# Second attention's keys and values projected inside the self-attention units, and token norms with one reciprocal root

## The chip, the cores and the metric

The kernel runs on one core of a Trainium2 chip. The core has a matrix engine (PE, with its weight loads shown as PEld), a vector engine (DVE), a scalar engine (ACT), a general engine (POOL), a synchronizing engine (SP) that here only issues transfers, and 16 DMA engines that all queues share. The metric is the device time of one execution in microseconds. Before the change it is 1516.2 us, the median of three runs from 1514.5 to 1518.3.

## What is computed

The input x is 16 batches of 128 tokens with 256 features; a context of the same shape comes with it. Four layers each add a gated branch to x, and each begins with a layer norm of x without weights:

```python
# first branch: gated attention over LN(x) (self) and over the context (cross)
ln_out = _ln(hidden_states, ln_w, ln_b)          # hidden_states is _layernorm(x): a norm of a norm
q = _ln(_fp8_linear_pertensor(ln_out, wq, ...))  # 16 heads of 128, 8 key groups; k, v likewise
core = _gqa(q, k, v)                             # self
xout = _gqa(qx, kx, vx)                          # cross: keys and values are cond @ w_kv_x
return catq(concat[core, xout]) @ wproj * ...
# second branch: feed-forward with ternary weights, silu(g) * u
# third branch: causal attention, 32 heads of 8, keys and values from the context
q = (Q @ w_q.T).reshape(B, S, G, HG, HD)         # G = 8 groups, HG = 4 heads, HD = 8
k = (K @ w_k.T).reshape(B, S, G, HD)             # 64 key features in all
v = (V @ w_v.T).reshape(B, S, G, HD)
# fourth branch: each token to one of 8 experts of bounded capacity
```

The keys and values of the third branch depend on the context and on weights only, not on x.

## The kernel before

The program has four stages, one after the other, which overlap at their seams.

**Gated attention.** The work is cut into 32 units: unit u is batch u % 16, the first 16 for self-attention and the last 16 for cross-attention. A loop over n runs from -11 to 135, and a unit advances by four steps. At each step the loop body issues parts of several units: projections of one unit (`project`, L422, into a ring of two PSUM banks, `ps_mm`), evictions by ACT (`evict`, L431 and L434), statistics of heads (`bn`, L443), the heads' reciprocal roots (`rstd`, L448 to L464), the heads' scaling by POOL (`mult`, L474), their transposes (`heads`, L485, L494), scores (L503, into a ring of two banks, `ps_sc`), their maxima (L511), exponentials (L519), the division (L527, L531), transposes and values (L539, L541, L549), the smoothing and rounding to eight bits (L560, and the helper `e4m3` whose last POOL step is L237 and whose result is called `cat`), and the output projection (`output`, L590). Weights are fetched in tiles called `stage` and split in two parts. The order on each engine is made by a scheduler that starts from this program order and moves an instruction ahead of others when its operands are ready earlier; so a part put at one place of the loop body can come to stand elsewhere on its engine.

Each self unit begins with a norm of its tokens. `stats` (L302 to L324) does the statistics of four batches at once, at n = -11, 5, 21 and 37. Since the reference takes a norm of a norm, it computes two reciprocal roots, the second from the variance that is left after the first, and multiplies them. A reciprocal root is made by `rsqrt` (L181 to L191): ACT takes the logarithm (L185) and an exponential of minus half of it (L186) as an estimate, and DVE improves that in four small steps (L187 to L190). All of its tiles lie in SBUF. The heads' reciprocal roots in `rstd` are made in another way: the estimate lies in a bank of the scores' PSUM ring and DVE needs three steps (L462 to L464).

Cross units fetch the context of their batch in `load` (L346) into a ring of two tiles, `ctx`.

**Feed-forward.** Four groups of four batches; `gate_up` and `down`. PE has no gaps here. SP fetches the weights of the next stage in these steps, among them `aq`, `ak`, `av`, `ao`.

**Second attention.** Groups of four batches. `front_step` spreads what a group needs over the steps before it: `load` (L931 to L945: the context of the group, called `cT`, issued on POOL's queue, and the mask, on SP's queue, from which DVE makes the tile `comb`), `norm`, `turn`, and then `qk` in four calls: two chunks of 128 query features and two chunks of 128 key features, each two matmuls of 128x512 (L982) and an ACT eviction (L987 for queries, L989 for keys). The key weights `ak` are laid out with every group's eight features repeated for its four heads, so the 64 key features fill 256 rows. For every batch `keys` masks the keys for four heads by POOL (L1000, result `kb`), projects the values with two matmuls (L1006) and writes them by four DVE copies (L1011) to a padded tile `vpad`, of which there are two; the zeros between stay from the start. A step of the main loop then makes eight heads' scores (L1022, L1029), maxima (L1036), exponentials (L1045), transposes (L1056, L1057) and, every second step, values (L1072) and their division (L1078, L1079); after a batch's last step the output projection (L1085). Routing of tokens to experts runs in between.

**Experts.** Eight of them, with transfers of their weights.

Of the change, these lines of the loop matter most: the place in the body behind which the new work is put.

```python
            if ab[1]:
                ab[1][0].project(ab[1][1])
                ab[1][0].evict(ab[1][1])
                ab[1][0].bn(ab[1][1])
            do(n, 5, "output")
```

Of the kernel before, what the change touches and what calls it, by code (L numbers as in the profile page):

```python
# [9 lines left out]
F32 = mybir.dt.float32  # L10
# [5 lines left out]
ALU = mybir.AluOpType  # L16
# [19 lines left out]
def flamingo_kernel(  # L36
# [206 lines left out]

    xqx = dram.tile([B, P, KD * P], F32, name="xqx")
    x1 = dram.tile([B, P, DM], F32, name="x1")
    NU = 2 * B


# [2 lines left out]
    with (  # L251
# [37 lines left out]
        def load_proj(cross, q):  # L289
# [7 lines left out]
                split(st, None, dst[:, c : c + n, 0, :], dst[:, c : c + n, 1, :])  # L297
            wpr[cross, q] = dst

        norms = {}  # L300

        def stats(g):  # L302

            xg = ap.tile([P, 4, DM], F32, tag="xg", name="xg", bufs=1)
            nc.sync.dma_start(
                out=xg, in_=x_in[4 * g : 4 * g + 4].rearrange("b s d -> s b d")
            )
            mv = small.tile([P, 4, 2], F32, tag="mv0", name="mv0", bufs=2)
            for j in range(4):
                stx = small.tile([P, 6], F32, tag="st0", name="st0")  # L310
                nc.vector.bn_stats(stx, xg[:, j, :])
                nc.vector.bn_aggr(mv[:, j, :], stx)
            v1 = small.tile([P, 4], F32, tag="v1", name="v1", bufs=1)
            nc.vector.tensor_scalar(v1, mv[:, :, 1], EPS, None, ALU.add)
            r1 = rsqrt(small, v1, 4, "x1", 1)
            v2 = small.tile([P, 4], F32, tag="v2", name="v2", bufs=1)
            nc.vector.tensor_tensor(v2, r1, r1, ALU.mult)
            nc.vector.tensor_tensor(v2, v2, mv[:, :, 1], ALU.mult)
            nc.vector.tensor_scalar(v2, v2, EPS, None, ALU.add)
            r2 = rsqrt(small, v2, 4, "x2", 1)  # L320
            rr = small.tile([P, 4], F32, tag="rr", name="rr", bufs=2)
            nc.vector.tensor_tensor(rr, r1, r2, ALU.mult)
            for j in range(4):
                norms[4 * g + j] = (xg[:, j, :], mv[:, j, 0:1], rr[:, j : j + 1])  # L324

        class Unit:
# [118 lines left out]
            def rstd(self):  # L445

                st = self.st
                var = small.tile([P, 24], F32, tag="q_var", name="q_var", bufs=1)  # L448
                dif = small.tile([P, 24], F32, tag="q_dif", name="q_dif", bufs=1)
                nc.vector.tensor_tensor(dif, st[:, :, 1], st[:, :, 4], ALU.subtract)  # L450
                nc.vector.scalar_tensor_tensor(dif, dif, 0.25, dif, ALU.mult, ALU.mult)
                nc.vector.scalar_tensor_tensor(
                    var, st[:, :, 2], P * EPS, st[:, :, 5], ALU.add, ALU.add
                )
                nc.vector.scalar_tensor_tensor(var, var, 1.0 / P, dif, ALU.mult, ALU.add)

                a = small.tile([P, 24], F32, tag="q_a", name="q_a", bufs=2)
                est = ps_sc([P, 24])
                self.r = small.tile([P, 24], F32, tag="q_r", name="q_r", bufs=2)
                nc.scalar.activation(a, var, AF.Ln)  # L460
                nc.scalar.activation(est, a, AF.Exp, scale=-0.5)
                nc.vector.scalar_tensor_tensor(a, est, -0.5, var, ALU.mult, ALU.mult)  # L462
                nc.vector.tensor_tensor(a, est, a, ALU.mult)
                nc.vector.scalar_tensor_tensor(self.r, a, 1.5, est, ALU.add, ALU.mult)  # L464

            def mult_q(self, c):
                self.mult(c + 2)
# [143 lines left out]
        units = [Unit(u) for u in range(NU)]  # L611


        loads = {}

        def at(n, f, *args):
# [34 lines left out]
        for n in range(first, last + 1):  # L651
            for m in range(0, B, 4):
                if n == 4 * m - 11:
                    stats(m // 4)
            once(n, -8, "load")
            for f, args in loads.get(n, ()):
                f(*args)
            ab = [front(n, i) for i in range(2)]
            do(n, 1, "recip")
            do(n, 4, "quant_last")  # L660
            do(n, 1, "divide")
            do(n, 0, "scores")
# [12 lines left out]
            for blk in range(2):  # L675
                once(n, -2, "mult", blk)
                once(n, -1, "heads", blk)
            do(n, -2, "mult_q")
            do(n, -1, "heads_q")
            do(n, 3, "quant")  # L680
            if ab[1]:
                ab[1][0].project(ab[1][1])
                ab[1][0].evict(ab[1][1])
                ab[1][0].bn(ab[1][1])
            do(n, 5, "output")
            once(n, 8, "residual")
# [197 lines left out]
    cq = f1.enter_context(tc.tile_pool(name="a1c", bufs=1, side="right", reuse_waits="tile"))  # L884
    gp = f1.enter_context(tc.tile_pool(name="a1f", bufs=2, side="right", reuse_waits="tile"))
    aq = cq.tile([P, KD, DM], F32, name="aq")
    ak = cq.tile([P, KD, DM], F32, name="ak")
    av = cq.tile([P, KD, NG * HD], F32, name="av")
    ao = cq.tile([P, KD, DM], F32, name="ao")
    bo = cq.tile([P, DM], F32, name="bo")  # L890
    nc.sync.dma_start(out=aq, in_=kpn(aqT))
    nc.sync.dma_start(out=ak, in_=kpn(akT))
    nc.sync.dma_start(out=av, in_=kpn(avT))
    nc.sync.dma_start(out=ao, in_=kpn(aoT))
    nc.sync.dma_start(out=bo, in_=b_o.partition_broadcast(P))

# [32 lines left out]
    front = {}  # L929

    def load(g):  # L931
        cT = gp.tile([P, KD, NT], F32, tag="cT", name="cT")
        nc.gpsimd.dma_start(out=cT, in_=kpn(ctxT)[:, :, g * NT : (g + 1) * NT])
        mi = gp.tile([P, NT], I32, tag="mi", name="mi", bufs=1)
        nc.sync.dma_start(
            out=mi, in_=mask[g * NT : (g + 1) * NT].partition_broadcast(P)
        )
        comb = gp.tile([P, G, P], BF16, tag="comb", name="comb")
        pad = gp.tile([P, NT], F32, tag="pad", name="pad", bufs=1)
        nc.vector.tensor_scalar(pad, mi, 0.0, NEG, ALU.is_equal, ALU.mult)  # L940
        nc.vector.tensor_tensor(
            comb, pad.rearrange("p (b t) -> p b t", b=G),
            causal[:, None, :].to_broadcast([P, G, P]), ALU.min,
        )
        front[g] = {"cT": cT, "comb": comb}  # L945

    def norm(g):
        rows = [x[b] for b in range(g * G, (g + 1) * G)]
# [22 lines left out]
            nc.scalar.copy(hT[:, k, :], pt.rearrange("p n t -> p (n t)"))  # L971
        front[g]["hT"] = hT

    def qk(g, i, c):

        f = front[g]
        if c == 0:
            f[i] = gp.tile([P, KD, NT], F32, tag="qk"[i], name="qk"[i] + "T")
        w, src = ((aq, f["hT"]), (ak, f["cT"]))[i]
        pm = psum.tile([P, NT], F32, tag="mm", name="ps_mm")  # L980
        for k in range(KD):
            nc.tensor.matmul(  # L982
                pm, w[:, k, c * P : (c + 1) * P], src[:, k, :],
                start=(k == 0), stop=(k == KD - 1),
            )
        if i == 0:
            nc.scalar.activation(f[i][:, c, :], pm, AF.Copy, scale=SCALE1)  # L987
        else:
            nc.scalar.copy(f[i][:, c, :], pm)  # L989

    kbs, vps, es, eTs, oTs, scs, mxs = {}, {}, {}, {}, {}, {}, {}

    def keys(b):

        g, j = divmod(b, G)
        f = front[g]
        tok = slice(j * P, (j + 1) * P)
        kb = ap.tile([P, KD, NQ, P], F32, tag="kb", name="kb")
        for c in range(KD):
            nc.gpsimd.tensor_tensor(  # L1000
                kb[:, c], f[1][:, c, None, tok].to_broadcast([P, NQ, P]),
                hmask[:, :, None].to_broadcast([P, NQ, P]), ALU.mult,
            )
        pm = psum.tile([P, NG, HD], F32, tag="mm", name="ps_mm")
        for k in range(KD):
            nc.tensor.matmul(  # L1006
                pm, f["cT"][:, k, tok], av[:, k, :], start=(k == 0), stop=(k == KD - 1)
            )
        vp = vpads[b % 2]
        for i in range(NQ):  # L1010
            nc.vector.tensor_copy(vp[:, :, i, HD * i : HD * i + HD], pm)  # L1011
        kbs[b], vps[b] = kb, vp

    def scores(n):

# [10 lines left out]
        with tc.high_priority(offset=100):  # L1026
            for i in range(2):
                rows = slice(32 * (2 * p + i), 32 * (2 * p + i) + 32)
                nc.tensor.matmul(  # L1029
                    s[:, i], f[0][rows, c, tok], kbs[b][rows, c], start=False, stop=True  # L1030
                )
        scs[n] = s

# [64 lines left out]
    def front_step(g, i):  # L1098

        if i == 0:  # L1100
            load(g)
            norm(g)
        elif i == 3:
            turn(g)
        elif 5 <= i < 9:
            qk(g, (i - 5) // 2, (i - 5) % 2)

    hds = {}
    for g in range(B // G):
# [182 lines left out]
```

## Time and profile before

| what | value |
|---|---|
| median of three runs | 1516.2 us (1514.5 to 1518.3) |
| the profiled execution | 1515.79 us, its span 1514.1 us |
| mean granted PE clock | 0.974 |
| busy: PE, DVE, ACT, POOL | 91%, 68%, 54%, 44% of the span |
| PE busy in 300 to 400 us (self-attention) | 91.92 us |
| PE busy in 560 to 900 us (cross-attention) | 333.13 us of 340 |
| PE busy in 960 to 1000 us (feed-forward) | 40.00 us |
| PE busy in 1200 to 1300 us (second attention) | 99.86 us |

The span is what the profiler saw from the first to the last instruction; the execution's time has a little around it. Busy time counts instructions at work, not waits. Where PE is busy all the time, what it does sets the pace; where it has gaps, some wait does, and the lists of waits say which. Rows of the profile name an engine, a line of the program, the operation, and the tiles written and read. The time that an instruction takes and the spacing to the next of its kind can differ, since matmuls overlap.

### The profile page before, as it was taken

To read this page: it belongs to the slowest core of one execution; us is meant where nothing else is said; L and a number is where in the kernel's file an instruction comes from. 1 tells how busy PE (TensorE), PEld (TensorE's weight loads), DVE (VectorE), ACT (ScalarE), POOL (GpSimd) and SP (SyncE) were. 2 spreads that over 40 slices of the span, in tenths; PEclk is the share of its full clock that TensorE was granted. 3 is DMA by queue.
4 is the path that set the end of the run, shared out by engine and by line. 5 is a ranking of instruction groups with operands and counts; after the bars stand their busy time and mean duration, and the time that the engine had idled before them with its cause. 6 is when DMAs were issued, how large, how long until landed. Compare 5 with 4: busy or idle time off the path is not lost. (4 is left out here: it accounts for less than half of the span.)

```text
span 1514.1 us, 24690 instructions
## 1 busy us (share of the span) xinstructions
PE 1381.9 (91%) x8612; PEld 1004.0 (66%) x8612; DVE 1022.1 (68%) x2756; ACT 810.6 (54%) x2421; POOL 672.7 (44%) x574
## 2 busy tenths in 40 slices
PE   2789899898988999999999987999999999996998
PEld 1477677677766777777777764555556565654887
DVE  8988878786887876767777664533678787882100
ACT  3666666666666766666666651543445454542121
POOL 4577676777667455565655553120121311111111
PEclk9799999999999999999999998999999999996999
DMA  4301001000031100000000006200300100012662
GB/s 120 118 8 32 15 15 32 11 19 15 22 91 50 49 26 11 18 15 18 15 15 19 5 8 194 61 0 0 112 22 8 50 9 36 9 40 66 202 195 64
DMA packets 51116, 68.69 MB, mean 45 GB/s; under 512 B 5291, under 2 KB 37739, under 8 KB 50992
## 3 DMA queue, kind: packets, MB, share of 16 engines
q1 hardware_dynamic: 36912, 41.31, 9.0%
q10 hardware_dynamic: 11456, 17.63, 3.6%
q0 software_dynamic: 2624, 8.16, 1.5%
q8 instruction: 69, 1.13, 0.3%
q14 instruction: 55, 0.45, 0.1%
HBM read 50.53 MB, written 16.81 MB: 44 GB/s over the span
## 5 line engine op out<-in xcount | busy, mean ns | idle before, releaser
L531 POOL TENSOR_TENSOR e<-e,sums 128x512 f32<-128x512 f32 x128 | 139.7, 1091 | 226.7 <-DVE sums L527 108.8
L474 POOL TENSOR_TENSOR raw<-raw,q_r 128x512 f32<-128x512 f32 x192 | 211.9, 1129 | 19.8 <-DVE q_r L464 18.9
L519 ACT ACTIVATE e<-ps_sc,mx 128x128 f32<-128x128 f32 x512 | 181.4, 369 | 65.0 <-DVE mx L511 56.5
L443 DVE BATCH_NORM_STATS2 q_st<-raw 128x6 f32<-128x128 f32 x768 | 174.0, 278 | 61.7 <-ACT raw L434 61.3
L1045 ACT ACTIVATE e<-ps_sc,mx 128x128 f32<-128x128 f32 x512 | 139.7, 383 | 117.5 <-DVE mx L1036 106.4
L590 PE MATMUL ps_acc<-wp,cat 128*128 128x512 f32 x512 | 159.4, 433 | 27.4 <-POOL cat L237 26.9
L237 POOL TENSOR_TENSOR cat<-e_t,e_e 128x1024 fp32r<-128x1024 bf16 x64 | 136.3, 2129 | 47.4 <-DVE e_t L231 47.4
L541 ACT COPY eT<-ps_tr 128x512 f32<-128x512 f32 x128 | 75.4, 589 | 151.7 <-PE ps_tr L539 151.6
L503 PE MATMUL ps_sc<-kT,qT 128*128 128x128 f32 x1024 | 140.4, 280 | 17.1 <-ACT qT L494 17.1
L503 PEld LDWEIGHTS ps_sc<-kT,qT 128*128 128x128 f32 x1024 | 131.0, 193 | 35.4 <-ACT qT L494 28.7
L1000 POOL TENSOR_TENSOR kb<-kT,hmask 128x512 f32<-128x512 f32 x32 | 33.6, 1068 | 243.8 <-PE ps_sc L1029 184.5
L590 PEld LDWEIGHTS ps_acc<-wp,cat 128*128 128x128 f32 x512 | 94.7, 191 | 69.6 <-POOL cat L237 35.9
L549 PE MATMUL ps_pv<-eT,vt 128*128 128x256 f32 x512 | 132.8, 381 | 1.0 <-DVE cat_y L560 1.0
L485 PE MATMUL ps_tr<-ident,raw 128*128 128x128 f32 x768 | 115.4, 277 | 16.1 <-POOL raw L474 14.2
L434 ACT COPY raw<-ps_mm 128x512 f32<-128x512 f32 x192 | 114.0, 594 | 26.6 <-PE ps_mm L422 24.1
L485 PEld LDWEIGHTS ps_tr<-ident,raw 128*128 128x128 f32 x768 | 91.9, 142 | 50.4 <-POOL raw L474 23.5
L549 PEld LDWEIGHTS ps_pv<-eT,vt 128*128 128x128 f32 x512 | 96.5, 190 | 31.5 <-issue 11.4
L560 DVE TENSOR_TENSOR cat_y<-ps_pv,r_sm 128x512 bf16<-128x512 f32 x128 | 86.9, 679 | 39.9 <-PE ps_pv L549 39.7
L511 DVE TENSOR_REDUCE mx<-ps_sc 128x4 f32<-128x512 f32 x128 | 87.1, 680 | 36.5 <-PE ps_sc L503 35.9
L494 ACT ACTIVATE qT<-ps_tr,hv 128x512 f32<-128x512 f32 x128 | 101.1, 790 | 17.5 <-PE ps_tr L485 15.5
L519 ACT ACTIVATION_READ_ACCUMULATOR e<-ps_sc,mx 128x1 f32 x512 | 105.7, 206 | 0.0
L1036 DVE TENSOR_REDUCE mx<-ps_sc 128x8 f32<-128x1024 f32 x64 | 78.1, 1221 | 25.6 <-PE ps_sc L1029 23.5
(227 smaller groups left out, 2769.0 us busy)
## 6 DMA issues: line engine op xcount, KB each, us to landing
w1t<-in_w ACTq DMA_DIRECT2D x8, 1024.0 KB, 5.1
w2t<-in_w ACTq DMA_DIRECT2D x8, 1024.0 KB, 5.5
disp<-empty SPq DMA_DIRECT2D x16, 257.0 KB, 8.3
xe<-disp SPq DMA_DIRECT2D x8, 514.0 KB, 3.6
stage<-in_wprojT SPq DMA_DIRECT2D x16, 256.0 KB, 2.8
xg<-in_x SPq DMA_DIRECT2D x4, 512.0 KB, 3.9
xb<-in_x SPq DMA_DIRECT2D x16, 128.0 KB, 2.0
ctx<-in_ctxT SPq DMA_DIRECT2D x16, 128.0 KB, 2.2
```

The costliest lines, as they stand in the source:

```text
L237: ins = nc.gpsimd.tensor_tensor(dst, t[:, part], e[:, part], ALU.subtract)
L434: nc.scalar.copy(raw.rearrange("p h d -> p (h d)"), pm)
L443: nc.vector.bn_stats(self.st[:, 4 * blk + j, :], self.raws[blk][:, j, :])
L474: ins = nc.gpsimd.tensor_tensor(src, src, self.r[:, 4 * blk : 4 * blk + 4, None].to_broadcast([P, 4, P]), ALU.mult,)
L485: nc.tensor.transpose(pt[:, j, :], src[:, j, :], ident)
L494: nc.scalar.activation(dst, pt, AF.Identity, scale=hv[:, col : col + 1], bias=hv[:, col + 1 : col + 2])
L503: nc.tensor.matmul(pscore[:, j, :], qT[:, j, :], self.kT[:, 2 * c + j // 2, :], start=True, stop=True,)
L519: nc.scalar.activation(e[:, j, :], pscore[:, j, :], AF.Exp, bias=self.mx[:, j : j + 1], accum_out=sums[:, j : j + 1],)
L531: nc.gpsimd.tensor_tensor(e, e, sums[:, :, None].to_broadcast([P, 4, P]), ALU.mult)
L549: nc.tensor.matmul(pv[:, 2 * g : 2 * g + 2, :], self.vt[:, gg * P : (gg + 1) * P], eT[:, 2 * g : 2 * g + 2, :], start=True, stop=True,)
L590: nc.tensor.matmul(self.acc, self.cat[c // 2][:, h % 8, :], wpr[self.cross, c][:, j, :, :], start=(h == 0), stop=(h == 15),)
L1045: nc.scalar.activation(e[:, i, :], s[:, i // NQ, i % NQ, :], AF.Exp, bias=mx[:, i : i + 1])
```

## The change

It has two parts.

The first concerns the third branch's keys and values. They are now projected in the self-attention loop, one batch per unit: `kv1(b)` is called at n = 4b + 3 (the last one at n = 61), between the second projection of the step and the output projection. It takes a buffer of `ps_mm`, multiplies the batch's context with 64 columns of `ak` (keys, 64x128 out) and with `av` (values, 128x64 out), lets ACT copy both to SBUF, and stores them to two new DRAM tensors, `k1s` and `v1s`. `load_kv1` fetches the batch's context four steps earlier, in the ring `ctx` that cross units use too; with the first one it fetches `ak` without the repetition, by two transfers that each read 8 of every 32 numbers, and `av`. In the second attention `load(g)` then reads the group's keys back with 16 transfers, which repeat them for the four heads on the way, and its values with one, all on SP's queue; the context's transfer on POOL's queue goes. The key half of `qk` goes (what is left is called `queries`), the values' matmuls and the four DVE copies of `keys` go, and one POOL copy per batch fills `vpad`.

The second concerns the token norms. The product of the two reciprocal roots is one reciprocal root, of var * (1 + EPS) + EPS * EPS. `stats` computes that and takes it with a new helper `rsqrt0`, which is what `rstd` did: logarithm, estimate in a bank of the scores' ring, three DVE steps. `rstd` calls the same helper and does the same as before. The function `rsqrt` stays in use elsewhere.

```diff
+        def rsqrt0(v, n, tag):
+            a = small.tile([P, n], F32, tag=f"{tag}_a", name=f"{tag}_a", bufs=2)
+            r = small.tile([P, n], F32, tag=f"{tag}_r", name=f"{tag}_r", bufs=2)
+            est = ps_sc([P, n])
+            nc.scalar.activation(a, v, AF.Ln)
+            nc.scalar.activation(est, a, AF.Exp, scale=-0.5)
+            nc.vector.scalar_tensor_tensor(a, est, -0.5, v, ALU.mult, ALU.mult)
+            nc.vector.tensor_tensor(a, est, a, ALU.mult)
+            nc.vector.scalar_tensor_tensor(r, a, 1.5, est, ALU.add, ALU.mult)
+            return r
...
-            v1 = small.tile([P, 4], F32, tag="v1", name="v1", bufs=1)
-            nc.vector.tensor_scalar(v1, mv[:, :, 1], EPS, None, ALU.add)
-            r1 = rsqrt(small, v1, 4, "x1", 1)
-            v2 = small.tile([P, 4], F32, tag="v2", name="v2", bufs=1)
-            nc.vector.tensor_tensor(v2, r1, r1, ALU.mult)
-            nc.vector.tensor_tensor(v2, v2, mv[:, :, 1], ALU.mult)
-            nc.vector.tensor_scalar(v2, v2, EPS, None, ALU.add)
-            r2 = rsqrt(small, v2, 4, "x2", 1)
-            rr = small.tile([P, 4], F32, tag="rr", name="rr", bufs=2)
-            nc.vector.tensor_tensor(rr, r1, r2, ALU.mult)
+            v = small.tile([P, 4], F32, tag="v1", name="v1", bufs=1)
+            nc.vector.tensor_scalar(v, mv[:, :, 1], 1.0 + EPS, EPS * EPS, ALU.mult, ALU.add)
+            rr = rsqrt0(v, 4, "x")
...
+        kv1_at = {4 * b + 3: b for b in range(B - 1)}
+        kv1_at[4 * (B - 1) + 1] = B - 1
+        def load_kv1(b):
+            if b == 0:
+                for k in range(KD):
+                    nc.sync.dma_start(
+                        out=ak[:, k].rearrange("p (g d) -> p g d", d=HD),
+                        in_=akT[k * P : (k + 1) * P, :].rearrange(
+                            "p (g h d) -> p g h d", h=NH // NG, d=HD
+                        )[:, :, 0, :],
+                    )
+                nc.sync.dma_start(out=av, in_=kpn(avT))
+            cxs[b] = ap.tile([P, KD, P], F32, tag="ctx", name="ctx")
+            nc.sync.dma_start(out=cxs[b], in_=kpn(ctxT)[:, :, b * P : (b + 1) * P])
+        def kv1(b):
+            cx = cxs.pop(b)
+            tok = slice(b * P, (b + 1) * P)
+            pm = ps_mm([P, P + NG * HD])
+            for k in range(KD):
+                nc.tensor.matmul(
+                    pm[: NG * HD, :P], ak[:, k, :], cx[:, k, :], start=(k == 0), stop=(k == KD - 1)
+                )
+            for k in range(KD):
+                nc.tensor.matmul(
+                    pm[:, P:], cx[:, k, :], av[:, k, :], start=(k == 0), stop=(k == KD - 1)
+                )
+            ko = ap.tile([NG * HD, P], F32, tag="ko", name="ko")
+            vo = ap.tile([P, NG * HD], F32, tag="vo", name="vo")
+            nc.scalar.copy(ko, pm[: NG * HD, :P])
+            nc.scalar.copy(vo, pm[:, P:])
+            nc.sync.dma_start(out=k1s[:, tok], in_=ko)
+            nc.sync.dma_start(out=v1s[tok, :], in_=vo)
...
+            if n + 4 in kv1_at:
+                load_kv1(kv1_at[n + 4])
+            if n in kv1_at:
+                kv1(kv1_at[n])
             do(n, 5, "output")
...
     def load(g):
-        cT = gp.tile([P, KD, NT], F32, tag="cT", name="cT")
-        nc.gpsimd.dma_start(out=cT, in_=kpn(ctxT)[:, :, g * NT : (g + 1) * NT])
+        tok = slice(g * NT, (g + 1) * NT)
+        kT = gp.tile([P, KD, NT], F32, tag="k", name="kT")
+        for r in range(0, P, HD):
+            q = r // 32
+            nc.sync.dma_start(
+                out=kT[r : r + HD],
+                in_=k1s.rearrange("(c q d) t -> q d c t", q=4, d=HD)[q][:, :, tok],
+            )
+        v = gp.tile([P, G, NG * HD], F32, tag="v", name="v")
+        nc.sync.dma_start(out=v, in_=v1s[tok, :].rearrange("(b t) n -> t b n", t=P))
...
-        pm = psum.tile([P, NG, HD], F32, tag="mm", name="ps_mm")
-        for k in range(KD):
-            nc.tensor.matmul(
-                pm, f["cT"][:, k, tok], av[:, k, :], start=(k == 0), stop=(k == KD - 1)
-            )
-        vp = vpads[b % 2]
-        for i in range(NQ):
-            nc.vector.tensor_copy(vp[:, :, i, HD * i : HD * i + HD], pm)
-        kbs[b], vps[b] = kb, vp
+        vp = vpads[b % 2][:]
+        nc.gpsimd.tensor_copy(
+            bass.AP(vp.tensor, vp.offset, [vp.ap[0], [P, NG], [32 + HD, NQ], [1, HD]]),
+            f["v"][:, j, :].rearrange("p (g d) -> p g d", d=HD)[:, :, None, :].to_broadcast(
+                [P, NG, NQ, HD]
+            ),
+        )
+        kbs[b], vps[b] = kb, vpads[b % 2]
```

The same step of the second attention that called `qk` for i = 5 to 8 now calls `queries` for i = 5 and 6.

More of the change, by code (lines that the diff above doesn't have):

```diff
@@ L245, in flamingo_kernel @@
     x1 = dram.tile([B, P, DM], F32, name="x1")
+    k1s = dram.tile([NG * HD, B * P], F32, name="k1s")
+    v1s = dram.tile([B * P, NG * HD], F32, name="v1s")
     NU = 2 * B
@@ L455, in rstd @@
                 nc.vector.scalar_tensor_tensor(var, var, 1.0 / P, dif, ALU.mult, ALU.add)
[L457 to L464, printed above, removed]
+                self.r = rsqrt0(var, 24, "q")
             def mult_q(self, c):
@@ L611, in flamingo_kernel @@
         units = [Unit(u) for u in range(NU)]
+        ak = ap.tile([P, KD, NG * HD], F32, tag="ak", name="ak", bufs=1)
+        av = ap.tile([P, KD, NG * HD], F32, tag="av", name="av", bufs=1)
+        cxs = {}
+        kv1_at = {4 * b + 3: b for b in range(B - 1)}
[30 more added lines that the diff above has]
+            nc.sync.dma_start(out=v1s[tok, :], in_=vo)
         loads = {}
@@ L886, in flamingo_kernel @@
     aq = cq.tile([P, KD, DM], F32, name="aq")
-    ak = cq.tile([P, KD, DM], F32, name="ak")
-    av = cq.tile([P, KD, NG * HD], F32, name="av")
     ao = cq.tile([P, KD, DM], F32, name="ao")
@@ L891, in flamingo_kernel @@
     nc.sync.dma_start(out=aq, in_=kpn(aqT))
-    nc.sync.dma_start(out=ak, in_=kpn(akT))
-    nc.sync.dma_start(out=av, in_=kpn(avT))
     nc.sync.dma_start(out=ao, in_=kpn(aoT))
@@ L944, in load @@
         )
-        front[g] = {"cT": cT, "comb": comb}
+        front[g] = {"k": kT, "v": v, "comb": comb}
     def norm(g):
@@ L972, in turn, with queries @@
         front[g]["hT"] = hT
-    def qk(g, i, c):
+    def queries(g, c):
         f = front[g]
         if c == 0:
-            f[i] = gp.tile([P, KD, NT], F32, tag="qk"[i], name="qk"[i] + "T")
-        w, src = ((aq, f["hT"]), (ak, f["cT"]))[i]
+            f["q"] = gp.tile([P, KD, NT], F32, tag="q", name="qT")
         pm = psum.tile([P, NT], F32, tag="mm", name="ps_mm")
@@ L982, in qk @@
             nc.tensor.matmul(
-                pm, w[:, k, c * P : (c + 1) * P], src[:, k, :],
+                pm, aq[:, k, c * P : (c + 1) * P], f["hT"][:, k, :],
                 start=(k == 0), stop=(k == KD - 1),
             )
[L986 to L989, printed above, removed]
+        nc.scalar.activation(f["q"][:, c, :], pm, AF.Copy, scale=SCALE1)
     kbs, vps, es, eTs, oTs, scs, mxs = {}, {}, {}, {}, {}, {}, {}
@@ L1000, in keys @@
             nc.gpsimd.tensor_tensor(
-                kb[:, c], f[1][:, c, None, tok].to_broadcast([P, NQ, P]),
+                kb[:, c], f["k"][:, c, None, tok].to_broadcast([P, NQ, P]),
                 hmask[:, :, None].to_broadcast([P, NQ, P]), ALU.mult,
             )
-        pm = psum.tile([P, NG, HD], F32, tag="mm", name="ps_mm")
-        for k in range(KD):
-            nc.tensor.matmul(
-                pm, f["cT"][:, k, tok], av[:, k, :], start=(k == 0), stop=(k == KD - 1)
-            )
-        vp = vpads[b % 2]
-        for i in range(NQ):
-            nc.vector.tensor_copy(vp[:, :, i, HD * i : HD * i + HD], pm)
-        kbs[b], vps[b] = kb, vp
+        vp = vpads[b % 2][:]
[6 more added lines that the diff above has]
+        kbs[b], vps[b] = kb, vpads[b % 2]
     def scores(n):
@@ L1029, in scores @@
                 nc.tensor.matmul(
-                    s[:, i], f[0][rows, c, tok], kbs[b][rows, c], start=False, stop=True
+                    s[:, i], f["q"][rows, c, tok], kbs[b][rows, c], start=False, stop=True
                 )
@@ L1104, in front_step @@
             turn(g)
-        elif 5 <= i < 9:
-            qk(g, (i - 5) // 2, (i - 5) % 2)
+        elif 5 <= i < 7:
+            queries(g, i - 5)
     hds = {}
```

## The prediction

> **What bounds the kernel now.** I read the page's engine shares first, then busy time by stretch of the span, then the waits of TensorE (PE) where it is not full, then the rows that the change touches. From the page:
>
> ```profile
> PE 1381.9 (91%) x8612; PEld 1004.0 (66%) x8612; DVE 1022.1 (68%) x2756; ACT 810.6 (54%) x2421; POOL 672.7 (44%) x574
> PE   2789899898988999999999987999999999996998
> DMA  4301001000031100000000006200300100012662
> ```
>
> PE is the bound on average, and the slices show where it is not: the start, the stretch to about 480 us (gated self-attention) and the turn near 910 us. Busy time by stretch (core's us: PE, PEld, DVE, ACT, POOL, clock, DMA):
>
> ```profile
> 300.00:400.00 100.00, 91.92 (x536) 76.79 (x536) 77.41 (x235) 65.16 (x206) 71.77 (x58) 1.00 0.05 17
> 960.00:1000.00 40.00, 40.00 (x124) 21.69 (x123) 18.98 (x65) 24.19 (x30) 5.85 (x6) 1.00 0.02 7
> 1200.00:1300.00 100.00, 99.86 (x1119) 61.88 (x1117) 82.35 (x169) 53.63 (x188) 15.67 (x15) 1.00 0.06 20
> ```
>
> In the ternary feed-forward and the second attention PE is full, so PE work removed there shortens the run nearly one for one. In self-attention 8% of PE's time is gaps, in which added PE work can lie. The gaps, by the waits of 100 to 420 us:
>
> ```profile
> PE ps_sc L503 <- ACT qT L494: 11.7, 13, 1.9
> PE ps_acc L590 <- POOL cat L237: 11.6, 11, 1.3
> PE ps_tr L485 <- POOL raw L474: 8.5, 16, 1.8
> ```
>
> From one scores chunk to the same chunk of the next unit a self unit takes 25.75 us, a cross unit 26.48 us (PE 99% busy there). Self units 3 and 4 take 28.75 and 26.80, units 7 and 8 the same: 4.0 us more than two plain ones, in the place of the norms of batches 8 to 11 and 12 to 15.
>
> **1. Second attention.** Removed from PE: 16 matmuls of keys (32 records) and 32 of values (64 records); from ACT 8 copies; from DVE 64 copies. Mean ns, from the rows of those tiles (min/median/max) and the timeline:
>
> ```profile
> L982 PE MATMUL ps_mm<-cT,ak x32: 592/592/697, 996.4 to 1276.6; 128*128 128x512 f32 x32
> L989 ACT COPY kT<-ps_mm x8: 586/586/587, 998.3 to 1277.2; 128x512 f32<-128x512 f32 x8
> L1006 PE MATMUL ps_mm<-av,cT x64: 219/275/323, 1055.2 to 1336.9; 128*128 128x64 f32 x64
> L1011 DVE COPY vpad<-ps_mm x64: 210/213/223, 1056.9 to 1338.6; 128x64 f32<-128x64 f32 x64
> 996.40 3.60 PE L982 MATMUL ps_mm<-cT,ak 128*128 128x512 f32 x8
> ```
>
> Records overlap, so spacing counts, not the mean: the two chunks of group 0 hold PE from 996.40 to 999.83, 3.43 us. The six others lie in steps of the second attention at 1269.98 to 1271.80 (1.82) and 1275.22 to 1277.00 (1.78), for example; 6 x 1.8 = 10.8 us. Below each is a floor: a pair of steps without any such filling has 7.0 us of PE work and takes 7.41 to 7.64, because the maxima, exponentials and transposes are late then. The steps that lose a chunk mostly keep an output projection or a query chunk, so I take 10.8, low end 8.4 (0.4 lost in each of six). The values' matmuls (0.39 us a batch) stand in just those short steps: a pair with them takes 7.41, without them 7.42 to 7.64, so in steady state they give nothing; only two early ones beside the last feed-forward projections count, 0.9 us (high end 16 x 0.39 = 6.2). Sum -3.4 -10.8 -0.9 = -15.1.
>
> Added: one POOL copy of 256 numbers per partition (128x256) a batch for the padded values. The trace has none. Bounds: 0.3 us and the 1.25 us of POOL's 128x256 normalization. I take 1.2, at no cost: POOL is 16% busy, the two buffers make it a batch (14.9 us) early, and only the value matmuls wait for it. If that cover went, 16 x 1.2 = 19 us. The loads: per group 16 key DMAs and one for values go out on SP ahead of the mask, 17 x 0.47 = 8 us. DVE waits for the mask at 952.70 now (0.85 us idle). The changed order has that DVE instruction after the third product of the feed-forward's second group, about 973, against a mask at about 957 + 8 = 965 at worst, so nothing.
>
> **2. Norms.** Per group of four batches DVE's small chain falls from 13 to 4 operations, ACT's from four to two, with one wait for DVE in place of two.
>
> ```profile
> L188 DVE TENSOR_TENSOR x_a<-x_a,v x8: 130/643/1486, 10.5 to 283.6; 128x4 f32<-128x4 f32 x8
> L189 DVE TENSOR_SCALAR x_a<-x_a x8: 155/726/973, 11.5 to 287.9; 128x4 f32<-128x4 f32 x8
> L463 DVE TENSOR_TENSOR q_a<-ps_sc,q_a x32: 160/182/183, 55.9 to 879.8; 128x24 f32<-128x24 f32 x32
> ACT e L519 <- DVE v L318: 5.2, 2, 2.6
> ```
>
> With all operands in SBUF these tiny operations take up to 1 us while POOL runs; with the estimate in PSUM the same step on 24 columns keeps to 160 to 183 ns. The Trainium skill ("SBUF — State Buffer", Who interferes with whom) says why: DVE with two SBUF inputs and POOL reading SBUF exclude each other. By that rule the new POOL copy in part 1, which reads SBUF, could hold up DVE sums there where the old PSUM copies could not; it gives no price, and no row shows this copy. The last line is ACT, held 2.6 us in the second and again in the third later group behind the second logarithm: that hold goes. Of the 4.0 us excess of these two groups I take 2.5 each (bounds 0 and 4.0: the statistics themselves stay), 2.0 for the second group (unit 1 takes 27.28, 1.5 over plain, and more lies in unit 0), and 2.5 at the start, where the chain runs from 9.07 to 15.67 and everything waits for its end (bounds 0 and 6). Late next at the start: POOL's rounding input (18.74) and the first projection (26.83), which also need weights. Sum -9.5, bounds 0 and -17. The estimate takes a buffer of the two-deep scores ring for about 1 us in four places: inside the bounds.
>
> **3. Keys and values in self units.** Per unit: 4 matmuls (8 records), 2 ACT copies, 3 DMAs on SP, one tenant more in the two-deep projection ring. PE: scores of 8 records 128x128 take 1.05 us, so 4 such are 0.52; with the 0.39 of values 0.91 us. They stand directly ahead of the output projection that waits for POOL's cat, where a plain unit shows
>
> ```profile
> 349.05 1.20 PE L590 MATMUL ps_acc<-wp,cat 128*128 128x512 f32 x4 [1.05 <-POOL cat L237]
> ```
>
> so 0.91 fits in 1.05. The ACT copies (nearest rows: 0.2 us for 24 columns, 0.37 for 128) come between the query eviction and the exponentials, where ACT is 65% busy. I take 0.25 us a unit, 4.0 in all, nearest to the row above. Bounds: 16 x (0.91 + 0.5) = 22.6 if nothing is hidden, and -2, since scores move ahead of a transpose in PE's order.
>
> **4. Junction with cross-attention** (units 13 to 16 take 117.68 us against 104 plain). The context loads of cross units now share two buffers with those of the new work: the second cross unit's waits for the first one's last use, a DMA of 2.2 us. Stores of keys and values stand on SP, waiting for ACT, ahead of the weight stages of cross-attention. I take +2 (-2 to +6; a load's latency three times).
>
> **5. Start.** The key weights come in two DMAs of 1024 runs of 32 bytes. Row for such runs:
>
> ```profile
> wgt<-in_w_gate SPq DMA_DIRECT2D x1, 8.0 KB, 1.7
> q1 hardware_dynamic: 36912, 41.31, 9.0%
> ```
>
> 256 runs landed in 1.7 us; the queue's packets take 9.0% x 16 x 1514 / 36912 = 59 ns. 2048 runs over 16 engines are 128 x 59 = 7.6 us at most, beside the first loads. Nothing waits for them before 40 us, but weights queue behind: stage loads are issued at 13.5. I take +1 (0 to 7.6). The Trainium skill ("DMA: Bandwidth & Descriptors", Specifications) wants at least 512 bytes per run and speaks against this load, without a price per run of 32 bytes.
>
> **Sum**: -15.1 -9.5 +4.0 +2 +1 = -17.6. The profiled execution took 1515.8 (span 1514.1), 0.4 below the median 1516.2 of runs from 1514.5 to 1518.3: 1498.2 on the first, 1498.6 on the second. I say 1498.4.
>
> **Rivals.**
> - A: the new work in self units is not hidden: PE alone 14.6 in place of 4.0 gives 1509; with the ACT copies 22.6 gives 1517, no change. For it: the wait for cat is not in every unit (11 in twelve, 11.6 us). Against: three kinds of gaps, 32 us in twelve units, 2.6 each.
> - B, slower: ACT is held. The copy of the new keys waits in ACT's queue for matmuls that PE does late, and the exponentials stand behind it. The trace has the price of a held ACT: 2.6 us, with the DVE chain, cost 4.0. A hold of a cat wait's length (1.3) and the copies make 1.8 a unit, 29 in all: 1523. It decides from 26 in all, 1.6 a unit. Against: half of PE's 1.05 wait would have to reach the exponentials of every unit.
> - C: the norms give nothing, since each start and unit is bound by something else: 1508.
> - D: the second attention keeps half its gain, bound by the floor of its chain: 1504.
>
> **Chances.** Forecast 0.46, D 0.10, C 0.12, A 0.20 (0.12 faster, 0.08 same), B 0.12. Faster by over 0.3% (4.5 us, about what can be told from no change) 0.80, same 0.08, slower 0.12. Range 1486 to 1514: below, the high ends of parts 1 and 2 together; above, A short of its worst; B and A's end are left out.
>
> **What shows it.** Right: no key or value matmuls after 990 us, the second attention about 11 us shorter; self units within 0.3 us of 25.75 with the wait for cat shrunk to 0.1 to 0.3; units 3+4 and 7+8 near 53; first projection near 24. Wrong: self units above 27, exponentials of ACT behind the key copy, a stall over 3 us at the first cross units, steps of the second attention no shorter than before.

## The result and the profile after

The changed kernel takes 1507.4 us, median of six runs from 1505.5 to 1509.8, against 1516.3 before (six runs). The ratio is 0.994, with a 95% interval of 0.9926 to 0.9954: 8.9 us faster, where 17.8 were forecast. The profiled execution took 1506.2 us, its span 1504.5.

The same lines of the page as were shown of before, now of the changed kernel:

```profile
PE 1379.0 (92%) x8644; PEld 1004.9 (67%) x8644; DVE 1014.0 (67%) x2656; ACT 811.2 (54%) x2437; POOL 677.6 (45%) x586
PE   2789899899988999999999997999999999996998
DMA  4301001000023100000000001600120100012652
```

PE's busy time has hardly moved (1381.9 to 1379.0): the matmuls went to another stage more than away. Where the time went can't be seen in shares, so I took marks that both traces have (the first score maximum of each unit and of each batch on DVE, the first silu of the feed-forward on ACT) and subtracted. Times in us, and "later" is the changed kernel's mark minus the other's:

| mark | before | changed | later |
|---|---|---|---|
| unit 0's first maximum | 63.96 | 60.34 | -3.6 |
| unit 2 | 111.50 | 108.78 | -2.7 |
| unit 13 | 403.89 | 406.02 | +2.1 |
| unit 17 | 521.57 | 532.12 | +10.6 |
| last maximum of the units | 906.54 | 918.93 | +12.4 |
| first silu | 935.58 | 949.00 | +13.4 |
| second attention, first maximum | 1057.39 | 1066.92 | +9.5 |
| second attention, last maximum | 1355.94 | 1346.87 | -9.1 |
| end of the span | 1514.1 | 1504.5 | -9.6 |

So the second half gained 22.5 us (13.4 + 9.1), half as much again as forecast (15.1), and the first half lost 13.4 where it was to gain 2.5 (9.5 from the norms less 7 in costs). Two sizes were off, in opposite directions.

In self-attention a plain unit (first maximum to first maximum) went from 25.74-25.86 us to 26.48-26.50. The waits of PE from 100 to 420 us, which were shown of before, are in the changed kernel:

```profile
PE ps_sc L504 <- ACT qT L495: 16.8, 11, 1.7
PE ps_tr L486 <- POOL raw L475: 9.7, 18, 2.0
```

(columns: us in all, times, longest.) The wait for POOL's cat, 11.6 us before, is gone from the list. The new work did fill that gap, as forecast. But the unit became longer all the same, and the wait for the transposed queries rose from 11.7 to 16.8. The timeline of PE at one such place, first before:

```profile
347.40 0.60 PE L485 MATMUL ps_tr<-ident,raw 128*128 128x128 f32 x4
349.05 1.20 PE L590 MATMUL ps_acc<-wp,cat 128*128 128x512 f32 x4 [1.05 <-POOL cat L237]
350.09 0.60 PE L539 MATMUL ps_tr<-ident,e 128*128 128x128 f32 x4
350.52 1.06 PE L503 MATMUL ps_sc<-kT,qT 128*128 128x128 f32 x8
351.34 1.18 PE L422 MATMUL ps_mm<-wq,xs 128*128 128x512 f32 x4
```

and in the changed kernel:

```profile
348.34 0.60 PE L486 MATMUL ps_tr<-ident,raw 128*128 128x128 f32 x4
348.87 0.65 PE L640 MATMUL ps_mm<-ctx,ak 128*64 128x128 f32 x4
349.45 0.66 PE L644 MATMUL ps_mm<-av,ctx 128*128 128x64 f32 x4
350.00 1.20 PE L591 MATMUL ps_acc<-wp,cat 128*128 128x512 f32 x4
351.04 1.05 PE L504 MATMUL ps_sc<-kT,qT 128*128 128x128 f32 x8
351.93 0.60 PE L540 MATMUL ps_tr<-ident,e 128*128 128x128 f32 x4
```

Each row gives its start, its duration, and in brackets an idle time before it. The new work stands without a gap up to the output projection, which starts 1.66 us after the transposes of the first row (348.34 to 350.00); in the kernel before, with nothing between, 1.65 (347.40 to 349.05). So the added work, 1.13 us from its first row to the output projection's (348.87 to 350.00; 0.91 was forecast), costs nothing here. What differs is the order behind: the scores now stand ahead of the transposes of the probabilities (tile e), which therefore start 1.93 us after the output projection in place of 1.04. The copy of the transposed probabilities by ACT, the values and DVE's smoothing all wait for these transposes. The scheduler turned the two round when the new work was put ahead of them. Whether that order, the work itself, or the transfers set the longer unit was to be found out.

### The profile page after: what moved, and what is told of

Its sections match the earlier page's. It is cut to its first block, busy times and chain, and to the rows that moved or that the text cites. A ratio compares the mean times of both kernels' runs of the same rounds, so it can differ in the third digit from the quotient of the medians.

```text
span 1504.5 us, 24887 instructions
## 1 busy us (share of the span) xinstructions
PE 1379.0 (92%) x8644; PEld 1004.9 (67%) x8644; DVE 1014.0 (67%) x2656; ACT 811.2 (54%) x2437; POOL 677.6 (45%) x586
## 3 DMA queue, kind: packets, MB, share of 16 engines
q0 software_dynamic: 2048, 6.07, 1.1%
q8 instruction: 69, 1.13, 0.3%
## 5 line engine op out<-in xcount | busy, mean ns | idle before, releaser
L591 PE MATMUL ps_acc<-wp,cat 128*128 128x512 f32 x512 | 160.5, 436 | 14.1 <-POOL cat L237 13.4
L550 PEld LDWEIGHTS ps_pv<-eT,vt 128*128 128x128 f32 x512 | 97.4, 192 | 31.5 <-issue 10.8
L1100 PEld LDWEIGHTS ps_tr<-ident,e 128*128 128x128 f32 x512 | 57.6, 140 | 58.1 <-ACT e L1089 21.7
L1045 POOL TENSOR_TENSOR kb<-kT,hmask 128x512 f32<-128x512 f32 x32 | 33.4, 1065 | 124.3 <-PE ps_sc L1073 119.2
```

Source lines behind the costliest of these rows:

```text
L550: nc.tensor.matmul(pv[:, 2 * g : 2 * g + 2, :], self.vt[:, gg * P : (gg + 1) * P], eT[:, 2 * g : 2 * g + 2, :], start=True, stop=True,)
L591: nc.tensor.matmul(self.acc, self.cat[c // 2][:, h % 8, :], wpr[self.cross, c][:, j, :, :], start=(h == 0), stop=(h == 15),)
```

## The experiments

Each kernel is timed beside the kernel before on the same chip; ratios are to that. The unit times are worked out from the marks as above.

**Norms alone (e1).** The kernel before with `stats` taken from the changed one and the keys and values left in the second attention:

```diff
-            r1 = rsqrt(small, v1, 4, "x1", 1)
...
-            r2 = rsqrt(small, v2, 4, "x2", 1)
...
+            rr = rsqrt0(v, 4, "x")
```

> Norms alone: the kernel before with the one reciprocal root of stats, keys and values left where they were. If the two parts add and the norms give what the changed kernel's trace suggests (first scores maximum 3.6 us earlier, units 3+4 and 7+8 some 2.0 us above two plain units instead of 4.0, so 1.6 to 2.0 each, about 1 in the second group), this gains 7 to 9 us: 1507 to 1509 us, and the moved keys and values are then worth about nothing net. Rival, the forecast's third case (norms give nothing): 1516 us. Plain self units stay at 25.75 us under both.

Measured: 1510.3 us against 1516.4, ratio 0.996 (0.9945 to 0.9975): 6.1 us, with an interval of 3.8 to 8.3. Its profiled run is 3.8 us above its median, so the sizes of parts are from the marks alone: unit 9 starts 4.6 us earlier than before; of that units 3 and 4 give 1.8 and units 7 and 8 another 1.8, and all before unit 3 gives 1.1. The first maximum came 3.5 us earlier and units 0 to 2 gave 2.4 back. The norms gain, less than expected of them, and plain units stay at 25.74 to 25.86. So the whole of the longer plain units is the other part's.

**The order, restored (e2).** The changed kernel, with the transposes issued ahead of the scores in the step that begins a unit:

```diff
-            do(n, 0, "scores")
-            do(n, 2, "probs")
+            if n % 4 == 0:
+                do(n, 2, "probs")
+            do(n, 0, "scores")
+            if n % 4:
+                do(n, 2, "probs")
```

> The changed kernel with one thing different: in the steps that begin a unit the transposes of probabilities are issued ahead of the scores, as the kernel before has them on PE; kv1 keeps its place and work. Order theory (a unit is longer because the scores now stand ahead of these transposes, so the copy of the transposed probabilities and all behind it come 0.95 us later): plain self units fall from 26.48 to at most 26.0 us and the whole by 6 us or more, 1501 us or less. Work theory (PE's 0.9 us per unit has no gap to lie in): units stay within 0.15 us of 26.48 and the whole within 2 us of 1507.4.

Measured: 1493.5 us, ratio 0.9854 (0.983 to 0.9879): 14 us under the changed kernel, with the same work. The timeline of PE at the same step:

```profile
372.18 0.65 PE L640 MATMUL ps_mm<-ctx,ak 128*64 128x128 f32 x4
372.76 0.66 PE L644 MATMUL ps_mm<-av,ctx 128*128 128x64 f32 x4
373.30 1.20 PE L591 MATMUL ps_acc<-wp,cat 128*128 128x512 f32 x4
374.34 0.60 PE L540 MATMUL ps_tr<-ident,e 128*128 128x128 f32 x4
374.78 1.06 PE L504 MATMUL ps_sc<-kT,qT 128*128 128x128 f32 x8
```

Plain self units take 25.74 to 25.76 (units 2, 10, 11; unit 6 25.94), as if the new work weren't there, and the wait for the transposed queries is back to 12.0 us. Two units, 5 and 9, take 27.88. The four units of the junction, 13 to 16, take 120.1 us: 126.1 in the changed kernel, 117.7 before. And the cross units, which no part of the change touches, went from 26.48 to 25.85, since the edit reaches them too. In plain units the work theory is out: the same work costs nothing with the order turned back. Units 5 and 9 are no such case: they are 2 us longer than with the norms alone (25.85), so over units 2 to 12 the edit gives back 3.8 of the 7.3 us by which the changed kernel is longer there (297.2 us, here 293.4, with the norms alone 290.0). The cross units had to be separated.

**The order, restored in self units only (e5).**

```diff
-            if n % 4 == 0:
+            if n % 4 == 0 and n < 4 * B:
```

(and the second condition as its opposite)

> As e2_transposes_first, but with the transposes ahead of the scores only while self units run; cross units keep the order of both the kernel before and the changed one. If the order is what cost the self units and the junction, and e2's shorter cross units (25.85 for 26.48) are a separate gift of the same edit: self units at 25.75 and units 13 to 16 at 120 as in e2, cross units at 26.48, the whole 8 us above e2: 1500 to 1503 us. Rival (the self units' gain in e2 came with the cross units' order): self units at 26.4 or more, the whole 1506 us or more.

Measured: 1501.1 us, ratio 0.9903 (0.9877 to 0.9928). Self units 25.74 to 25.95 with the same two exceptions, units 13 to 16 120.8 us, cross units 26.48. So the order is worth about 6 us where the change upset it (by the marks 9.1 between units 2 and 17, less 3.4 that units 0 and 1 of this trace lose), and the rest of e2's gain is the cross units'.

**The same edit on the kernel before (e6).**

> The kernel before with the same edit as e2. Its self units have that order already, so only cross units should change, 13 of them by 0.63 us: 1516.3 - 8 = 1508 us. If the new order needs what the change brings, nothing changes: 1516 us.

Measured: 1508.0 us, ratio 0.9939 (0.9917 to 0.9961). Cross units 25.85, self units unchanged. Beside it the kernel before took 1518.2, so the kernel before had some 9 us to gain (6 to 13 by the interval) by turning two rows round in its cross units; the marks show 7.0 of them between units 17 and 30.

**The order, spoilt in the kernel before (e9).** No new work at all; in self units the transposes are made to stand behind the next unit's scores:

```diff
+                    if c == 2 and j == 0 and u < B:
+                        stay_after(ins, units[u].scored)
```

> The kernel before, with no new work in its units, and with one thing turned round in self units: at the step that begins a unit the scores stand ahead of the transposes of probabilities, as in the changed kernel. Order theory: plain self units lengthen from 25.75 to 26.4 to 26.5 us without any added work, eleven of them by 0.7, and the junction (units 13 to 16, 117.7 us) by 2 to 6; the whole 1525 to 1532 us. Work theory: units stay at 25.75 and the whole within 2 us of the kernel before.

Measured: 1531.5 us, ratio 1.0088 (1.0071 to 1.0105): 13.6 us slower by the order alone. Plain self units take 27.1 to 27.6. That is more than the expected 26.4 to 26.5, while the junction, units 13 to 16, grows by 1.6 us (119.2), less than the expected 2 to 6. More than the one pair moved: two matmuls of the next projection now stand ahead of the scores as well, so that the transposes start 2.39 us after the output projection (1.93 in the changed kernel, 1.04 before). With the new work absent, the wait for cat stays and another appears. Its waits of PE from 100 to 420 us:

```profile
PE ps_tr L485 <- POOL raw L474: 23.1, 21, 2.8
PE ps_acc L595 <- POOL cat L237: 7.6, 8, 1.1
PE ps_sc L503 <- ACT qT L494: 4.6, 4, 1.3
```

The wait for POOL's scaled heads (tile raw) rose from 8.5 to 23.1; where PE waits for it at 354.25 us (1.76), POOL itself had started on it only at 353.16, after waiting 1.71 us for DVE's reciprocal roots (q_r). The size of the penalty thus depends on the rest of the order; that the order costs time without any new work is shown.

**A context ring of its own (e3).**

```diff
-            cxs[b] = ap.tile([P, KD, P], F32, tag="ctx", name="ctx")
+            cxs[b] = ap.tile([P, KD, P], F32, tag="cx1", name="cx1")
```

> The changed kernel with the new work's contexts in a ring of their own, so that the first cross units' contexts don't wait for it. Ring theory (forecast's part 4): units 13 to 16, 126.1 us in the changed kernel against 117.7 before, come back by 4 us or more, the whole to 1503 us or less. Rival (the junction is longer because two more pieces of the new work and their stores stand among the new weights' preparation): units 13 to 16 stay within 1.5 us of 126.1, the whole within 1.5 us of 1507.4.

Measured: 1505.6 us, ratio 0.9931 (0.9909 to 0.9952); units 13 to 16 125.0 us. It gains 1 of the 8.4 us, not 4: the shared ring, which the forecast named, is not what makes the junction long.

**All of it at the start (e4).**

```diff
-            if n in kv1_at:
-                kv1(kv1_at[n])
+            if -7 <= n < 1:
+                for b in range(2 * (n + 7), 2 * (n + 7) + 2):
+                    kv1(b)
```

(loads two steps earlier, a context ring of four)

> The changed kernel with all sixteen batches' keys and values projected in the first steps of the program (two a step from the seventh step before the first unit's scores), where PE was busy for 25 of the first 60 us, with a context ring of four. If the cost of the new work is its place in the units: plain self units return to 25.75 us (14 x 0.7 = 10 us) and units 13 to 16 to about 118 us (8 us), less what the start loses: 15 us of PE work and 2 MB of contexts among the first weights, 3 to 12 us. The whole 1492 to 1500 us. If the place is not the cause (the transfers or the PSUM ring's tenant are), units stay at 26.4 to 26.5 us and the whole is 1507 us or more.

Measured: 1509.8 us, ratio 0.9954 (0.9942 to 0.9966). Units are back at 25.75 and the junction at 117.7, but the first maximum comes at 79.3 us in place of 60.3: 19 us lost, more than the 3 to 12 expected. The matmuls are slower there: those of the keys here, and those of the keys in the changed kernel's units, are

```profile
L638 PE MATMUL ps_mm<-cx,ak x64: 272/421/476, 8.5 to 84.1; 128*64 128x128 f32 x64
L640 PE MATMUL ps_mm<-ctx,ak x64: 272/273/324, 76.3 to 484.7; 128*64 128x128 f32 x64
```

(ns, shortest, median, longest.) Up to about 70 us a piece holds PE for 2.1 us, not for the 1.1 of the units, though the granted clock is shown as 1.00 there too; the trace doesn't say why. The 14 pieces that stand ahead of the first maximum take 28 us of PE, where 15 were expected for all 16. The wait for the first context, PE's longest (8.5 us), cost nothing: the first projection starts at 23.75 us, in the changed kernel at 26.59. Out of the units the new work costs them nothing, then, but this other place is no better.

**Keys only (e7).** The values stay in the second attention, with the context loaded on POOL's queue and DVE's copies as before:

```diff
+        cT = gp.tile([P, KD, NT], F32, tag="cT", name="cT")
+        nc.gpsimd.dma_start(out=cT, in_=kpn(ctxT)[:, :, g * NT : (g + 1) * NT])
...
+                pm, f["cT"][:, k, tok], av[:, k, :], start=(k == 0), stop=(k == KD - 1)
...
+            nc.vector.tensor_copy(vp[:, :, i, HD * i : HD * i + HD], pm)
```

> The changed kernel with only the keys moved; values are projected in the second attention with the context loaded as before, and copied by DVE from PSUM. From the first maximum of the second attention to the last the kernel before takes 298.6 us, the changed one 280.0: 18.6 less, where 11.7 were forecast. If the keys' matmuls alone are worth the forecast's 1.8 us a chunk: 298.6 - 10.8 = 287.8 or so here, and the values (0.39 us of PE and 0.85 of DVE a batch) the other 7. If the keys are worth more than their chunks (ACT's copies and the context's transfer went too): 283 or less, and the values little. Self units keep the order with the scores first: 26.1 to 26.5 us. The whole 1510 to 1516 us in the first case, 1504 to 1509 in the second.

Measured: 1514.5 us, ratio 0.9973 (0.9959 to 0.9987). From the second attention's first maximum to its last 287.8 us, against 298.6 before and 280.0 with both moved. By this trace the six key chunks are worth 10.8 us, what was worked out for them, and the values 7.8, where 0.9 were forecast. That the first agrees to the tenth is luck: traces of kernels with the same second attention differ by more (296.8 to 298.6 us where nothing is moved, 279.5 to 283.1 where both are). With these ends the keys are worth 9.0 to 10.8 and the values 4.7 to 8.3.

**The values' copies back on DVE (e8).**

```diff
-        nc.gpsimd.tensor_copy(
...
+        for i in range(NQ):
+            nc.vector.tensor_copy(
+                vp[:, :, i, HD * i : HD * i + HD],
+                f["v"][:, j, :].rearrange("p (g d) -> p g d", d=HD),
+            )
```

> The changed kernel with the padded values written by four DVE copies a batch from SBUF in place of the one POOL copy; all matmuls as in the changed kernel. DVE theory (the extra 7 us of the second attention came from DVE, which bounds its busier steps): the second attention returns to 284 to 287 us, the whole to 1511 to 1514. PE theory (they came from the values' matmuls): 280 to 281, the whole within 1.5 us of 1507.4.

Measured: second attention 280.1 us, the same as with POOL; the whole 1509.5, ratio 0.994 (0.9916 to 0.9963), the ratio of the changed kernel. DVE theory falls: the 64 copies are back (186 ns each, median) and cost nothing. The values' gain comes with the values' matmuls, with what PE's order is without them, or with the context's transfer, which went too; these weren't told apart.

**Both orders pinned (e10).** As e2, and in a unit's third step the transposes are made to stand behind the scores; in e2 the units 5 and 9 alone had those turned round.

```diff
+                    if c == 0 and j == 0:
+                        stay_after(ins, self.scored)
```

> As e2, with the order of the third step pinned as well: there the scores stand ahead of the transposes in every unit. In e2 units 5 and 9 had these two the other way round and took 27.88 us. If that order is the cause they fall to 25.8 us and the whole is 3 to 4 us under e2's 1493.5: 1488 to 1491 us. If those two units are long for another reason (the norms of the next batches fall there), no change.

Measured: 1484.9, 1489.2 and 1490.3 us, ratio 0.9799 (0.9776 to 0.9821). But units 5 and 9 still take 27.88 and 28.00: the expectation fails at the place that it named, although the total falls into its range. Its profiled run, 1490.3, is no faster than that of e2, 1488.0. Why the total is lower I can't say from the traces. Why those two units are long wasn't tested; with the norms alone (e1) they take 25.85. Their traces show one more pair turned round, this one on ACT: the exponentials of a chunk stand ahead of the copy of the transposed queries, and the scores wait for that copy. In unit 9, which starts at 297.97:

```profile
306.46 0.37 ACT L520 ACTIVATE e<-ps_sc,mx 128x128 f32<-128x128 f32 x1 [1.25 <-DVE mx L512]
307.85 0.79 ACT L495 ACTIVATE qT<-ps_tr,hv 128x512 f32<-128x512 f32 x1
308.69 1.16 PE L504 MATMUL ps_sc<-kT,qT 128*128 128x128 f32 x8 [0.52 <-ACT qT L495]
```

and in unit 11, a plain one, which starts at 351.71:

```profile
359.66 0.78 ACT L495 ACTIVATE qT<-ps_tr,hv 128x512 f32<-128x512 f32 x1 [0.72 <-PE ps_tr L486]
360.34 0.36 ACT L520 ACTIVATE e<-ps_sc,mx 128x128 f32<-128x128 f32 x1
361.27 1.05 PE L504 MATMUL ps_sc<-kT,qT 128*128 128x128 f32 x8
```

The scores of unit 9 wait 1.8 us in all for such copies, those of a plain unit 0.7. Units 5 and 9 have this order in e2, e5, e10 and e11, and not in the changed kernel.

**No new work in the junction (e11).** As e10, with the last three batches as second ones in units 10 to 12:

```diff
-        kv1_at = {4 * b + 3: b for b in range(B - 1)}
-        kv1_at[4 * (B - 1) + 1] = B - 1
+        kv1_at = {4 * b + 3: [b] for b in range(B - 3)}
+        for b in range(B - 3, B):
+            kv1_at[4 * b - 9].append(b)
```

> As e10, with the last three batches' keys and values projected as second ones in units 10 to 12, so that none falls in the junction, units 13 to 16. If the new work there is what is left of the junction's cost (120.1 us in e2, 117.7 before), those units fall to 118 us and units 10 to 12 lengthen by at most 0.9 each: 0 to 2.5 us under e10. If the second pieces find no gap, units 10 to 12 take 26.7 us and nothing is gained.

Measured: 1486.8 us, ratio 0.98 (0.9784 to 0.9816): 31 us under the kernel before, some 20 under the changed one, and not to be told from e10. Units 13 to 16 take 117.4 us, and units 10 to 12 are 1.07 us longer each: 26.81, 26.82 and 27.73, where e10 has 25.74, 25.74 and 26.66. A first piece was hidden by the wait for cat; a second one passes in full. What the junction gained (3.3 us) these units lost (3.2): from unit 2 to unit 17 both kernels take 414.0 us. The expectation's second case came true, and nothing is gained.

## Why the prediction was right or wrong

The sign and the range were right (1507.4 in 1486 to 1514), the size by half: 17.8 us were forecast, 8.9 came. That the total lay in the range is in part luck, since two large misses, of opposite sign, half cancelled. It also came within 2 us of two rivals' times, A's 1509 and C's 1508; C (the norms give nothing) is wrong all the same, since they gave 6.1 (e1). Of the forecast's own signs of being right, self units within 0.3 us of 25.75 failed. By its own parts:

1. **Second attention, -15.1 forecast.** By the marks -3.9 up to its first maximum and -18.6 from there. Group 0's two chunks were to give 3.4, and with the keys alone (e7) the stretch from the first silu to this maximum is 3.4 shorter; the six others gave their 10.8 within what such traces vary by (9.0 to 10.8). The mis-sized term is the values: 0.9 was taken, with a high end of 6.2, and 7.8 came (4.7 to 8.3). The step that failed is that the values' matmuls "stand in just those short steps" that a chain limits. That reading came from plain batches, and there it holds: batches 4, 8 and 12 take 16.0 us with and without. Batches with norms, routing or the last feed-forward work in them are longer than that, and there it fails: between keys only and both moved, batches 0, 1 and 5 shorten by 1.2, 1.7 and 2.5. Those are more than PE's 0.39 a batch; e1 has 20.5 for batch 5 with nothing of this moved, against 22.1 before, so some of it varies without the change; that this is the order in which the routing falls is likely, not shown. The new POOL copy measured 0.40 us (median), a third of what was taken:

```profile
L1050 POOL COPY vpad<-v x16: 388/398/931, 991.8 to 1323.5; 128x256 f32<-128x256 f32 x16
```

   The mask's landing cost nothing: the list of waits has none of DVE for it after the change, though the 17 transfers do stand ahead of it.

2. **Norms, -9.5 forecast.** 6.1 came in the medians (e1), 4.6 up to unit 9 in the trace. Where the estimate lies in PSUM, the three DVE steps were never lengthened, though POOL was at work beside 11 of the 12:

```profile
L310 DVE SCALAR_TENSOR_TENSOR x_a<-ps_sc,v x4: 152/158/163, 9.7 to 297.6; 128x4 f32<-128x4 f32 x4
L311 DVE TENSOR_TENSOR x_a<-ps_sc,x_a x4: 149/156/163, 10.2 to 297.8; 128x4 f32<-128x4 f32 x4
L312 DVE SCALAR_TENSOR_TENSOR x_r<-x_a,ps_sc x4: 157/157/158, 10.4 to 298.0; 128x4 f32<-128x4 f32 x4
```

   163 ns at most, where the steps in SBUF took up to 1486 beside POOL and 130 to 170 with POOL idle. That agrees with the Trainium skill's rule on two SBUF inputs that the forecast cited ("SBUF — State Buffer", Who interferes with whom). That rule alone doesn't cover L189, which reads one tile and took up to 973 as well. The later groups gave 1.8 each for a forecast of 2.5, and the start gave back most of its 3.5 in units 0 to 2.

3. **New work in self units, +4.0 forecast; the failed step.** Against the norms alone, units 2 to 12 take 7.3 us more (297.2 for 290.0). The hiding was right in plain units: the work lies in the wait for cat and costs nothing when the order holds (e2, e5), though it is 1.13 us and not 0.91. What failed is the bound "-2, since scores move ahead of a transpose in PE's order". The forecast had seen the new order and priced it as a possible gain. In plain units it is the whole cost: undone, it gives all 0.7 us of each back (e2, e5), and without any new work such an order makes them 1.4 us longer (e9). It isn't the whole of the 7.3: 3.8 came back with it, and nearly all the rest is units 5 and 9, which then take 2 us more than with the norms alone. The forecast's rival A would have the right size (14.6 on PE; 7.3 and, in part 4, 8.1 were lost), for a reason that e2 excludes in plain units; rival B, ACT held, isn't seen: the copies of keys wait 0.3 us.

4. **Junction, +2 forecast with ends -2 and +6.** Units 13 to 16 lost 8.1 against the norms alone, outside the bounds. Of that the order is 5.3 (e5: 120.8), the rest is the new work that lies there (e11: 117.4 without it). The shared ring, for which the forecast charged, is 1.1 (e3).

5. **Start, +1.** Nothing: with and without the key weights' short runs the first maximum comes at 60.34 and 60.43. The term's high end, 7.6 us, took 59 ns a run from the queue's average packet; in the trace the 2048 packets of 32 bytes run from 7.16 to 8.71 us, 9 ns each (median). The Trainium skill asks for at least 512 bytes for the full rate ("DMA: Bandwidth & Descriptors", Specifications). The trace agrees, since packets of 1024 bytes took 46 ns, six times the bytes per ns of the short ones; but for 64 KB that loss is small.

By part, then: +7.3 and +8.1, against the norms alone, in place of +4 and +2 for the moved work, and -22.5, against the kernel before, in place of -15.1 where it had been; what is left of the difference to the total (unit 30 and the passage to the feed-forward, +2.9 against the kernel before) also occurs in kernels without the move (unit 30 takes 28.8 us in e1 and 28.7 in e9, which has no part of the change), so it isn't counted to the change.

## What to carry to other kernels

Work that fits in a gap of an engine was free here only where it left the order behind the gap as it was. A scheduler that decides by readiness can turn neighbours round when something is put in front of them, on other engines too, so compare the orders and price each swapped pair by who waits for it: a pair whose first half feeds other engines is not a detail, and its cost can be tested by swapping it in the old kernel too, if the trace is then read for what else moved. A reading that "these matmuls are hidden here" holds for the steps from which it was read; look at the busiest steps of the stage as well as at the plain ones.

## What the runs showed that I had not expected

Self units of the changed kernel and cross units take the same 26.48 us, though their work differs, and both take 25.75 to 25.85 with the transposes first: the pair's order, not PE's load, made the difference in both. The cross units looked full at 98% PE busy (333.13 of 340 us; the forecast read 99), and still lost 0.63 us each to the order; a busy share near one was no proof of a bound there.
